# Two-layer graph network on one core: layer 1's products with swapped operands, a constant added by a matrix product, norms by pairs, full-width loads in the sign pass

## The chip, the core and the metric

One core of one Trainium2 chip runs the whole program. The time is device microseconds (us) from launch to end. Three runs of the kernel before gave 795.92, 791.58 and 790.1 us: the median is 791.58 us.

The engines go by their short names: PE (TensorE; its weight loads are shown apart as PEld), DVE (VectorE), ACT (ScalarE), POOL (GpSimd), and SP, which issues plain DMAs. A matrix product has a stationary operand, which is loaded into PE, and a moving operand, whose columns stream through it. "128\*65 128x128 f32" in a group line is a product whose stationary operand is 128 rows by 65 columns and whose moving operand is 128 by 128. A float32 product of this kernel leaves two records in the trace.

## The reference

2708 nodes with 256 features; `adj` is sparse (about 0.3% of its entries and the diagonal are not zero, the first rows and columns hold most). Two layers, each followed by `layernorm(x + layer(x))`:

```
layer 0:  for each of 3 heads: hW = h @ W; e = leaky_relu of sums of hW over neighbours
          att = softmax over j of (e[j] where adj[i, j] > 0); out += (att * adj) @ hW
          two GRU cells (edge, node) on adj @ h and on the mean of the heads;
          result = diag(adj) * (edge cell + node cell)
layer 1:  h = (x @ W) as n x 4 heads x 64
          e[i, j, head] = leaky_relu(s_src[i, head] + s_dst[j, head])   where adj[i, j] > 0.5
          alpha = softmax over i;   out[j] = sum over i of alpha[i, j, head] * h[i, head] + bias
```

A destination j without any entry over 0.5 gets the plain mean over all i: that is what the softmax gives when all its entries are masked alike.

## The kernel before, in words

**Order.** Each operation is first only noted (`Order.add`, lines 100-104) as a node of a graph; nodes held by `together()` stay in one piece. `issue` (line 230) then works out an order for all five engines by a list schedule: a cost in us for each node (`duration`, line 182), a forward pass (line 293) that starts the node of best rank on whichever engine is free first, a backward pass that makes new ranks, and then `tries` = 200 random shifts of ranks, of which the best planned span is kept. In the forward pass a PE node costs twice its duration if it starts between 62 and 146 us, and 1.35 times if it belongs to layer 1 (line 324). The best order is written out; each engine runs its own list strictly in that order. Gathers on POOL are also tied to an operation that the plan has ending shortly before them (lines 406-422).

**Sign pass (0 to about 140 us).** The transposed adjacency is loaded in three column parts (2048 up, 1024 to 2047, 0 to 1023), 22 row blocks each, through a ring of five buffers. ACT writes signs as 8-bit floats into `m8` (22 rows of 2708 bytes per partition, tile f_big); DVE writes "over 0.5" flags (`over`, tile f_wts); PE turns flags into bits (line 956) and multiplies blocks of `m8` with 9 or 18 columns of numbers (`source_products`, line 748). The last column block has only 20 nodes, so its stationary operand has 20 columns.

**Layer 0 (to about 625 us).** For each of six groups of 512 destinations, in the order 4, 3, 2, 1, 0, 5: gathered rows are multiplied and summed, then `cells_and_norm` (line 1193) runs the GRU cells, the norm, writes x1 to X1 (tile f_low), adds it to the running sum `xacc` (line 1271), and writes rows of h, exponentials and bits to the table T1.

**Layer 1 (from about 630 us).** Destinations are cut into 32 pieces (BLOCKS1) 32, 64 or 128 wide. Each has up to 7 lists of 128 sources (tiles). POOL gathers each tile's 128 rows from T1 (`fetch_h`, 96 gathers; a ring of five items of up to three tiles). `layer1` (line 1447) makes a mask (DVE), the weights q = max(S * factor, 1) * mask (the first product on ACT if the piece is 128 wide and its block b is odd, else on DVE; the rest on DVE), and for each tile and head one product: stationary h with a column of ones (65 columns), moving q (32, 64 or 128 columns). So the sums stand with 65 features on the partitions and destinations along the row, in one of three banks `acc`. Of the 104 tiles, 48 are 128 wide, 32 are 64, 23 are 32 and one is 20 wide. When a block of 128 destinations is complete, `finished` (line 1495) adds `hm`, the tiny multiple of the mean of h (four ACT copies, tile f_big), turns the block around with four transposes into a bank `side`, divides by the sum of weights (DVE reciprocal; the multiplication on DVE for odd b, on ACT for even b), adds x1, takes mean and variance, then square root (ACT), reciprocal and shift (DVE), the scaling (ACT), and stores the block. `hm` comes from `xacc` by two small sets of products (lines 1384-1399).

Of the kernel before, what the change touches and what calls it, by code (L numbers as in the profile page):

```python
# [13 lines left out]
F8 = mybir.dt.float8e4  # L14
# [9 lines left out]
P = 128  # L24
# [64 lines left out]
class Order:  # L89
# [3 lines left out]
    def __init__(self, nc, tc):  # L93
        self.tc = tc
        self.nc, self.nodes, self.open, self.held, self.holds = nc, [], None, (), {}
        self.stage, self.stages, self.second, self.tries = None, {}, 1 << 30, 200
        for e in ("tensor", "vector", "scalar", "gpsimd", "sync"):
            setattr(self, e, _Queue(self, e))
# [83 lines left out]
    def duration(self, call):  # L182
# [30 lines left out]
        return 0.45  # L213

    def holds_port(self, call):
# [14 lines left out]
    def issue(self, cross=0.12, pace=0.6, rate=345.0e3, land=2.0, chained=(), turns=12):  # L230
# [55 lines left out]
        port = [self.holds_port(calls[0]) for calls in nodes]  # L286
        gather = [calls[0][1] == "indirect_dma_start" for calls in nodes]
        before = [[] for _ in range(count)]
        for n in range(count):
# [3 lines left out]
        def forward(rank):  # L293
# [11 lines left out]
            for _ in range(count):  # L305
# [82 lines left out]

        chance = random.Random(1)
        parts = sorted(s for s in self.stages if s)  # L390
        for again in range(self.tries):
            moved = list(ahead)
            for part in chance.sample(parts, 3):
                by = chance.uniform(-25.0, 25.0)
                for n in self.stages[part]:
                    moved[n] += by
            rank = [-b - a + chance.uniform(-2.0, 2.0) for b, a in zip(backward(*best[2:]), moved)]
# [49 lines left out]
def fast_path(ctx: ExitStack, tc: tile.TileContext, i: dict, out: bass.AP, bad: bass.AP):  # L447
# [70 lines left out]

    big = Arena("f_big", NB * N)
    wts = Arena("f_wts", 2 * 2 * KD * 3 * D * 4)  # L520
# [173 lines left out]

    G.memset(m8[:, last, :].bitcast(U32), 0)
    G.memset(over_last.bitcast(U32), 0)
# [51 lines left out]
    def source_products(k, bl, lo, hi, end=False):  # L748

        with R.together():  # L750
            for b in bl:
                T.matmul(
                    both[: size[b], b * 2 * H3 + lo : b * 2 * H3 + hi], lhsT=m8[:, k, cols(b)], rhs=u_e[:, k, lo:hi],
                    start=not both_begun[0], stop=end, skip_group_check=True,
                )
                both_begun[0] = True
# [175 lines left out]
    for g, (c0, c1) in enumerate(parts):  # L932
        w = c1 - c0
        b0, b1 = c0 // P, -(-c1 // P)
        for k in range(NB):
# [436 lines left out]
    most = 3  # L1372
    o_ring = Ring([big.take([C65, HEADS1, P], at=4096 + n * 2048) for n in range(2)])
    S_ring = Ring([big.take([P, HEADS1, CH], at=a) for a in (40960, 12288, 28672)])
# [4 lines left out]
    )  # L1379
    hm = home("f_hm", [C65, HEADS1])  # L1380
    V.memset(hm, TINY)
    xm = home("f_xm", [P, KD])
    pm1 = side.next()
# [8 lines left out]
    with R.together():  # L1392
        for h in range(HEADS1):
            for k in range(KD):
                T.matmul(
                    pm2[:C1, h : h + 1], lhsT=w1[:, k, h * C1 : (h + 1) * C1], rhs=xm[:, k : k + 1],
                    start=(k == 0), stop=(k == KD - 1), skip_group_check=True,
                )
    V.tensor_scalar(hm[:C1], pm2[:C1, :HEADS1], TINY, None, op0=MUL)

# [46 lines left out]
    def layer1(j):  # L1447
# [29 lines left out]
        if begin:  # L1477
            outs[b] = acc.next()
            x1b_of[b] = xb_ring.next()
            Q.dma_start(x1b_of[b][: size[b]], X1[b * P : b * P + size[b], :])  # L1480
# [512 lines left out]
```

## Time and profile before

| what | value |
|---|---|
| median of three runs | 791.58 us |
| the profiled execution, its own time | 797.94 us |
| its span, first to last instruction | 796.2 us |
| busy: PE, DVE, POOL, ACT | 652.9, 550.3, 420.3, 261.9 us |
| mean granted PE clock | 0.882 |
| PE busy in 200 to 600 us | 390 of 400 us |
| PE, DVE, POOL, ACT busy in 628 to 782 us | 113.7, 115.2, 103.2, 78.8 of 154 us |

How to read it: each group line gives what one kind of instruction took in all (busy), the mean length of one in ns, and the idle time of its engine just before it with what ended that. The length of one PE record overlaps its neighbours, so prices are taken from whole runs of records (length of the run over its count) or from busy time over count. "PEclk" is the share of PE's full clock that was granted. All operations of the fast path carry line 417, the line that writes the order out, so they are told apart by tile and shape.

### The profile page before, as it was taken

To read this page: it belongs to the slowest core of one execution; us is meant where nothing else is said; L and a number is where in the kernel's file an instruction comes from. 1 tells how busy PE (TensorE), PEld (TensorE's weight loads), DVE (VectorE), ACT (ScalarE), POOL (GpSimd) and SP (SyncE) were. 2 spreads that over 40 slices of the span, in tenths; PEclk is the share of its full clock that TensorE was granted. 3 is DMA by queue.
4 is the path that set the end of the run, shared out by engine and by line. 5 is a ranking of instruction groups with operands and counts; after the bars stand their busy time and mean duration, and the time that the engine had idled before them with its cause. 6 is when DMAs were issued, how large, how long until landed. Compare 5 with 4: busy or idle time off the path is not lost.

```text
span 796.2 us, 12355 instructions
## 1 busy us (share of the span) xinstructions
PE 652.9 (82%) x4212; PEld 467.0 (59%) x4212; DVE 550.3 (69%) x1383; ACT 261.9 (33%) x621; POOL 420.3 (53%) x528
## 2 busy tenths in 40 slices
PE   1786554669999999989999999999998786866763
PEld 1785444555456656565557576574458685755763
DVE  8477798669357968487796455885256585787795
ACT  4436554001113301142114111141225214635775
POOL 5012725546665666576665666763001557777780
PEclk9998555579999999999999999999999756877796
DMA  8888997471114223133213422242004544576541
GB/s 279 327 266 247 320 298 245 144 213 47 39 27 120 77 83 83 42 82 97 53 32 116 126 64 47 54 109 61 1 0 172 195 126 131 180 213 173 142 120 58
DMA packets 60820, 103.68 MB, mean 130 GB/s; under 512 B 20913, under 2 KB 37201, under 8 KB 60109
## 3 DMA queue, kind: packets, MB, share of 16 engines
q1 hardware_dynamic: 40511, 61.62, 23.6%
q0 software_dynamic: 17472, 41.15, 19.9%
q8 instruction: 35, 0.57, 0.3%
q10 hardware_dynamic: 2766, 0.04, 0.2%
q14 instruction: 36, 0.29, 0.1%
HBM read 93.28 MB, written 12.27 MB: 133 GB/s over the span
## 4 chain that ended last, share of the span: by engine, by line
PE 59%; DVE 15%; issue 5%; DMA 5%; ACT 4%; another core or an unknown queue 2%; POOL 1%; SPq 0%; DVEq 0%; ACTq 0%; POOLq 0%
PE side L417 37%; PE acc L417 18%; DVE f_lists L417 4%; ACT f_big L417 3%; DVE f_big L417 3%; DMA f_wts<-in_adjT_dram 3%; PE lst L417 2%; DVE f_low L417 1%; DVE f_raw L417 1%; DMA f_lists<-f_T,f_idx 1%; DVE f_wts L417 1%; DVE f_xT L417 1%; DMA f_xg__139<-f_T,f_idx 1%; SPq L417 0%
## 5 line engine op out<-in xcount | busy, mean ns | idle before, releaser
L417 POOL DMA_INDIRECT f_lists<-f_T,f_idx x96 | 112.6, 1173 | 113.8 <-DMA f_low<-f_X 62.6
L417 POOL DMA_INDIRECT f_raw<-in_adjT_dram,f_idx x115 | 128.5, 1118 | 78.0 <-issue 39.5
L417 PE MATMUL side<-f_xT,f_wts 128*128 128x512 f32 (+1 forms) x288 | 120.6, 544 | 2.6 <-ACT f_big L417 2.6
L417 PE MATMUL side<-f_big,f_wts 128*128 128x512 f32 (+1 forms) x288 | 120.4, 542 | 0.0
L417 PE MATMUL acc<-f_xT,f_lists 128*65 128x128 f32 (+2 forms) x560 | 69.4, 294 | 17.4 <-DVE f_xT L417 13.3
L417 PEld LDWEIGHTS side<-f_big,f_wts 128*128 128x128 f32 x288 | 52.3, 190 | 53.3 <-issue 53.1
L417 PEld LDWEIGHTS side<-f_xT,f_wts 128*128 128x128 f32 x288 | 51.5, 190 | 48.3 <-issue 43.8
L417 PEld LDWEIGHTS acc<-f_xT,f_lists 128*65 128x65 f32 x560 | 65.1, 183 | 20.7 <-DVE f_xT L417 15.4
L417 ACT ACTIVATE f_big<-f_wts 128x1024 fp8e4<-128x1024 f32 (+1 forms) x66 | 60.8, 950 | 39.6 <-DMA f_wts<-in_adjT_dram 26.1
L417 ACT ACTIVATE f_big<-side,f_biases 128x512 f32<-128x512 f32 (+1 forms) x48 | 30.5, 636 | 112.3 <-PE side L417 98.4
L417 PE MATMUL side<-f_pow,f_wts 128*128 128x8 bf16 x484 | 23.8, 170 | 47.3 <-DVE f_wts L417 45.6
L417 PE MATMUL side<-f_big,f_gat_w 128*128 128x512 f32 (+1 forms) x144 | 56.1, 543 | 1.3 <-DVE f_s_d L417 1.3
L417 DVE TENSOR_SCALAR f_wts<-f_wts 128x1024 fp8e4<-128x1024 f32 (+1 forms) x66 | 42.7, 659 | 18.7 <-PE side L417 10.3
L417 PEld LDWEIGHTS <-f_wts 128*128 128x128 fp8e4 x484 | 20.2, 106 | 51.8 <-DVE f_wts L417 48.0
L417 POOL DMA_INDIRECT f_xg__139<-f_T,f_idx x33 | 34.9, 1058 | 27.4 <-issue 7.7
L417 DVE TENSOR_TENSOR f_lists<-f_iota,f_lists 128x2816 f16<-128x2816 f16 (+5 forms) x26 | 48.4, 1862 | 0.6
L417 POOL DMA_INDIRECT f_xg__138<-f_T,f_idx x32 | 36.4, 1137 | 23.3 <-issue 9.0
L417 POOL DMA_INDIRECT f_xg__137<-f_T,f_idx x36 | 35.3, 982 | 25.2 <-issue 9.2
L417 DVE TENSOR_TENSOR f_big<-f_big 128x512 f32<-128x512 f32 (+1 forms) x48 | 30.1, 627 | 24.4 <-ACT f_big L417 22.8
L417 PE MATMUL lst<-f_lists 128*128 128x256 f16 (+4 forms) x285 | 37.8, 296 | 10.0 <-DVE f_lists L417 10.0
L417 POOL DMA_INDIRECT f_xg__140<-f_T,f_idx x30 | 32.6, 1087 | 22.8 <-PE acc L417 8.8
L417 ACT COPY f_big<-acc 128x104 f32<-128x104 f32 (+8 forms) x51 | 12.6, 246 | 95.5 <-PE acc L417 78.5
(260 smaller groups left out, 1275.2 us busy)
## 6 DMA issues: line engine op xcount, KB each, us to landing
f_wts<-in_adjT_dram SPq DMA_DIRECT2D x42, 512.0 KB
f_wts<-in_adjT_dram SPq DMA_DIRECT2D x21, 330.0 KB
f_big<-f_Rd SPq DMA_DIRECT2D x5, 1024.0 KB
f_big<-f_Sd SPq DMA_DIRECT2D x5, 1024.0 KB
f_T<-f_ah SPq DMA_DIRECT2D x21, 132.0 KB
f_X<-f_low SPq DMA_DIRECT2D x21, 128.0 KB
f_low<-f_X SPq DMA_DIRECT2D x21, 128.0 KB
out_dram<-f_big SPq DMA_DIRECT2D x21, 128.0 KB
```

The costliest lines, as they stand in the source:

```text
L417: made[n] = getattr(getattr(self.nc, engine_), method)(*args, **kw)
```

## The change

Six edits, the diff cut to what they do:

1. The planner: PE nodes that start before 160 us cost twice only if an operand of over 48 columns moves (a float32 column counts as 128); layer 1 costs 1.2 times; 280 tries instead of 200, with other random shifts.
2. `m8` gets 108 bytes behind its last row, zeroed with the first 128 columns of every row, and stationary operands of the last column block are read 128 columns wide, over the row's end into the next row. The same for `over`. Rows of the result past the 20th are not used.
3. Layer 1's products change sides: q is stationary (32, 64 or 128 columns) and h with its ones (65 columns) moves. The sums then stand with destinations on the partitions.
4. `hm` becomes one row of 260 numbers, made by two products with one stationary column; it is put into the bank by a first product with a row of ones before a block's other products. The four ACT copies and the four transposes go, and `finished` reads the bank directly.
5. The first multiplication of q goes to ACT for 128-wide pieces with b not divisible by 3, instead of odd b.
6. Square root, reciprocal and shift of the norm are made for two blocks at once (the last four singly); scaling and storing of an even block wait for its neighbour.

```diff
@@ Order
-        self.stage, self.stages, self.second, self.tries = None, {}, 1 << 30, 200
+        self.stage, self.stages, self.second, self.tries = None, {}, 1 << 30, 280
+    def columns(call):
+        moving = call[3]["rhs"] if call[1] == "matmul" else call[2][1]
+        return _size(moving) * (128 if _width(moving.dtype) == 4 else 1)
+        slow = [1.0 + any(self.columns(c) > 48 for c in calls) if e == "tensor" else 1.0 for e, calls in zip(engine, nodes)]
-                    took[n] = busy[n] * (2.0 if 62.0 < t < 146.0 else 1.35 if n >= self.second else 1.0)
+                    took[n] = busy[n] * (slow[n] if t < 160.0 else 1.2 if n >= self.second else 1.0)
-            for part in chance.sample(parts, 3):
-                by = chance.uniform(-25.0, 25.0)
+            wide = chance.choice((3.0, 10.0, 30.0))
+            fine = chance.choice((0.2, 1.0, 4.0))
+            for part in chance.sample(parts, chance.randint(0, 4)):
+                by = chance.uniform(-1.0, 1.0) * wide
@@ sign pass
+    m8_flat = big.take([P, NB * N + SPARE], F8, at=0)
-    G.memset(m8[:, last, :].bitcast(U32), 0)
+    G.memset(m8_flat[:, last * N :].bitcast(U32), 0)
+    G.memset(m8[:, :, : (SPARE + 127) // 128 * 128].bitcast(U32), 0)
-                    both[: size[b], ...], lhsT=m8[:, k, cols(b)], rhs=u_e[:, k, lo:hi],
+                    both[:, ...], lhsT=m8_flat[:, k * N + b * P : k * N + (b + 1) * P],
-                        pb[: size[b], o : o + 8], lhsT=over[:, b * P - c0 : b * P - c0 + size[b]], rhs=pow16,
+                        pb[:, o : o + 8], lhsT=over[:, b * P - c0 : (b + 1) * P - c0], rhs=pow16,
@@ layer 1
-        for h in range(HEADS1):
-            for k in range(KD):
-                T.matmul(pm2[:C1, h : h + 1], lhsT=w1[:, k, h * C1 : (h + 1) * C1], rhs=xm[:, k : k + 1], ...)
-    V.tensor_scalar(hm[:C1], pm2[:C1, :HEADS1], TINY, None, op0=MUL)
+        for k in range(KD):
+            T.matmul(pm2[:1, :D], lhsT=xm[:, k : k + 1], rhs=w1[:, k, :D], start=(k == 0), stop=(k == KD - 1))
+    V.tensor_scalar(hm.rearrange(...)[:, :, :C1], pm2[:1, :D].rearrange(...), TINY, None, op0=MUL)
-        if w == P and b % 2 == 1:
+        if w == P and b % 3:
             outs[b] = acc.next()
+            T.matmul(outs[b][: size[b], :H65], lhsT=ones[:, : size[b]], rhs=hm, start=True, stop=False, ...)
-                        o[:C65, h * P + p0 : h * P + p0 + w], lhsT=hg[:, m, h * C65 : (h + 1) * C65],
-                        rhs=q[:, h, m, :], start=(begin and m == 0 and h == 0),
+                        o[p0 : p0 + w, h * C65 : (h + 1) * C65], lhsT=q[:, h, m, :],
+                        rhs=hg[:, m, h * C65 : (h + 1) * C65], start=False,
@@ finished
-        oc = o_ring.next()
-        for h in range(HEADS1):
-            S.activation(oc[:, h, :p], o[:C65, h * P : h * P + p], AF.Identity, bias=hm[:, h : h + 1])
-        pt = side.next()
-        with R.together():
-            for h in range(HEADS1):
-                T.transpose(pt[:p, h * C65 : (h + 1) * C65], oc[:, h, :p], ident[:C65, :C65])
-        got = pt[:p, :H65].rearrange("p (h c) -> p h c", h=HEADS1)
+        got = o[:p, :H65].rearrange("p (h c) -> p h c", h=HEADS1)
-        S.activation(rstd[:p, b : b + 1], mv[:p, b, 1:2], AF.Sqrt, bias=eps[:p])
-        V.reciprocal(rstd[:p, b : b + 1], rstd[:p, b : b + 1])
-        V.scalar_tensor_tensor(nmr[:p, b : b + 1], mv[:p, b, 0:1], -1.0, rstd[:p, b : b + 1], op0=MUL, op1=MUL)
-        S.activation(y, y, AF.Identity, bias=nmr[:p, b : b + 1], scale=rstd[:p, b : b + 1])
-        Q.dma_start(out[b * P : b * P + p, :], y)
+        waiting.append((b, y))
+        if b % 2 == 0 and b < last - 3:
+            return
+        rstds(waiting[0][0], b + 1)
+        for c, v in waiting:
+            S.activation(v, v, AF.Identity, bias=nmr[: size[c], c : c + 1], scale=rstd[: size[c], c : c + 1])
+            Q.dma_start(out[c * P : c * P + size[c], :], v)
+        waiting.clear()
```

More of the change, by code (lines that the diff above doesn't have):

```diff
@@ L213, in duration @@
         return 0.45
+    @staticmethod
+    def columns(call):
+        moving = call[3]["rhs"] if call[1] == "matmul" else call[2][1]
+        return _size(moving) * (128 if _width(moving.dtype) == 4 else 1)
     def holds_port(self, call):
@@ L387, in issue @@
             rank = [-b - a for b, a in zip(backward(when, took), ahead)]
-        chance = random.Random(1)
+        chance = random.Random(3)
         parts = sorted(s for s in self.stages if s)
@@ L392, in issue @@
             moved = list(ahead)
-            for part in chance.sample(parts, 3):
-                by = chance.uniform(-25.0, 25.0)
+            wide = chance.choice((3.0, 10.0, 30.0))
+            fine = chance.choice((0.2, 1.0, 4.0))
+            for part in chance.sample(parts, chance.randint(0, 4)):
+                by = chance.uniform(-1.0, 1.0) * wide
                 for n in self.stages[part]:
                     moved[n] += by
-            rank = [-b - a + chance.uniform(-2.0, 2.0) for b, a in zip(backward(*best[2:]), moved)]
+            rank = [-b - a + chance.uniform(-fine, fine) for b, a in zip(backward(*best[2:]), moved)]
             for turn in range(3):
@@ L517, in fast_path @@
     X1 = dram.tile([N, D], F32, name="f_X1")
-    big = Arena("f_big", NB * N)
+    SPARE = (NB * P - N + 3) // 4 * 4
+    big = Arena("f_big", NB * N + SPARE)
     wts = Arena("f_wts", 2 * 2 * KD * 3 * D * 4)
@@ L692, in fast_path @@
     early = ah_all[:, : early_n * 64].rearrange("p (s i) -> p s i", i=64)
-    G.memset(m8[:, last, :].bitcast(U32), 0)
+    G.memset(m8_flat[:, last * N :].bitcast(U32), 0)
+    G.memset(m8[:, :, : (SPARE + 127) // 128 * 128].bitcast(U32), 0)
+    for over in over_ring.slots:
+        G.memset(over.bitcast(U32)[:, (N - parts[0][0]) // 4 // 32 * 32 :][:, :32], 0)
     G.memset(over_last.bitcast(U32), 0)
@@ L752, in source_products @@
                 T.matmul(
-                    both[: size[b], b * 2 * H3 + lo : b * 2 * H3 + hi], lhsT=m8[:, k, cols(b)], rhs=u_e[:, k, lo:hi],
+                    both[:, b * 2 * H3 + lo : b * 2 * H3 + hi], lhsT=m8_flat[:, k * N + b * P : k * N + (b + 1) * P],
+                    rhs=u_e[:, k, lo:hi],
                     start=not both_begun[0], stop=end, skip_group_check=True,
@@ L1372, in fast_path @@
     most = 3
-    o_ring = Ring([big.take([C65, HEADS1, P], at=4096 + n * 2048) for n in range(2)])
     S_ring = Ring([big.take([P, HEADS1, CH], at=a) for a in (40960, 12288, 28672)])
@@ L1379, in fast_path @@
     )
-    hm = home("f_hm", [C65, HEADS1])
+    hm = home("f_hm", [1, H65])
     V.memset(hm, TINY)
+    ones = home("f_ones", [1, P])
+    V.memset(ones, 1.0)
     xm = home("f_xm", [P, KD])
@@ L1392, in fast_path @@
     with R.together():
-        for h in range(HEADS1):
-            for k in range(KD):
[L1395 to L1398, printed above, removed]
-    V.tensor_scalar(hm[:C1], pm2[:C1, :HEADS1], TINY, None, op0=MUL)
+        for k in range(KD):
+            T.matmul(pm2[:1, :D], lhsT=xm[:, k : k + 1], rhs=w1[:, k, :D], start=(k == 0), stop=(k == KD - 1))
+    V.tensor_scalar(
+        hm.rearrange("p (h c) -> p h c", h=HEADS1)[:, :, :C1], pm2[:1, :D].rearrange("p (h c) -> p h c", h=HEADS1),
+        TINY, None, op0=MUL,
+    )
     lists.reset()
@@ L1478, in layer1 @@
             outs[b] = acc.next()
+            T.matmul(
+                outs[b][: size[b], :H65], lhsT=ones[:, : size[b]], rhs=hm, start=True, stop=False,
+                skip_group_check=True,
+            )
             x1b_of[b] = xb_ring.next()
@@ L1518, in finished @@
         stats(y, p, b)
-        S.activation(rstd[:p, b : b + 1], mv[:p, b, 1:2], AF.Sqrt, bias=eps[:p])
-        V.reciprocal(rstd[:p, b : b + 1], rstd[:p, b : b + 1])
-        V.scalar_tensor_tensor(nmr[:p, b : b + 1], mv[:p, b, 0:1], -1.0, rstd[:p, b : b + 1], op0=MUL, op1=MUL)
-        S.activation(y, y, AF.Identity, bias=nmr[:p, b : b + 1], scale=rstd[:p, b : b + 1])
-        Q.dma_start(out[b * P : b * P + p, :], y)
+        waiting.append((b, y))
[3 more added lines that the diff above has]
+        for c, v in waiting:
+            S.activation(
+                v, v, AF.Identity, bias=nmr[: size[c], c : c + 1], scale=rstd[: size[c], c : c + 1]
+            )
+            Q.dma_start(out[c * P : c * P + size[c], :], v)
+        waiting.clear()
+    waiting = []
     dn_ring = Ring([home(f"f_dn{n}_", [P, HEADS1]) for n in range(2)])
```

## The prediction

> **What bounds the kernel now.** First the page's slices of the span:
>
> ```profile
> PE   1786554669999999989999999999998786866763
> DVE  8477798669357968487796455885256585787795
> POOL 5012725546665666576665666763001557777780
> PEclk9998555579999999999999999999999756877796
> DMA  8888997471114223133213422242004544576541
> ```
>
> A slice is 19.9 us. In the first seven the adjacency loads set the pace (DMA 8 to 9 tenths) and PE's clock falls to half. In slices 11 to 30 PE is full at full clock: layer 0's work, which the change leaves alone. From slice 32 on no engine is full: layer 1, where the change lies. So I read that stage by itself, cut where the width of the pieces changes (PE, PEld, DVE, ACT and POOL busy us, granted clock, DMA share, GB/s):
>
> ```profile
> 630.00:660.00 30.00, 27.07 (x251) 26.33 (x249) 18.64 (x55) 6.30 (x17) 16.70 (x16) 0.57 0.42 115
> 660.00:676.00 16.00, 9.39 (x96) 8.38 (x94) 11.10 (x30) 8.24 (x24) 11.60 (x11) 0.69 0.56 149
> 676.00:702.00 26.00, 19.43 (x149) 18.16 (x150) 20.68 (x34) 14.66 (x52) 19.11 (x16) 0.86 0.55 165
> 702.00:728.00 26.00, 15.55 (x138) 13.81 (x137) 17.93 (x49) 12.94 (x45) 18.36 (x18) 0.66 0.74 217
> 728.00:782.00 54.00, 40.31 (x308) 38.02 (x307) 45.39 (x96) 36.29 (x128) 36.44 (x26) 0.85 0.45 128
> ```
>
> Narrow pieces (32 and 64 wide) run to 676: PE bounds their first half, at 0.57 of its clock. Then come blocks 3 to 6 (128 wide), 7 to 10 (64 wide), 11 to 20 (128 wide, 5.4 us a block), with PE, DVE and POOL at 67 to 84%. The stage's groups:
>
> ```profile
> L417 POOL DMA_INDIRECT f_lists<-f_T,f_idx x96 | 112.6, 1173 | 113.8 <-DMA f_low<-f_X 62.6 <-issue 16.7 <-PE acc L417 11.7
> ...
> L417 PE MATMUL acc<-f_xT,f_lists 128*65 128x128 f32 x272 | 40.0, 312 | 10.8 <-DVE f_xT L417 8.8 <-issue 1.9
> ...
> L417 ACT ACTIVATE f_big<-acc,f_hm 65x128 f32<-65x128 f32 x84 | 24.2, 362 | 43.7 <-PE acc L417 32.0 <-remote 11.3 <-issue 0.4
> ...
> L417 PE MATMUL side<-f_ident,f_big 65*128 65x65 f32 x84 | 13.5, 268 | 14.8 <-ACT f_big L417 11.0 <-issue 3.6
> ```
>
> Gathers take 1.17 us and stand 0.30 us apart where nothing else holds them: 96 of them need 141 us, and they run from 611.5 to 775.2, 164 us. POOL is the nearest bound, with about 22 us of other waits, of which PE's products are 11.7.
>
> **What a product costs by its two operands.** PE's timeline gives it:
>
> ```profile
> 641.16 2.90 PE L417 MATMUL acc<-f_raw,f_lists 128*65 128x64 f32 x24 [0.94 <-DVE f_raw L417]
> 643.85 1.90 PE L417 MATMUL acc<-f_xT,f_lists 128*65 128x64 f32 x16
> ...
> 651.41 1.87 PE L417 MATMUL side<-f_xm,f_w 128*64 128x1 f32 x16
> 653.20 3.73 PE L417 MATMUL acc<-f_xT,f_lists 128*65 128x32 f32 x32
> ```
>
> All this but the end of the second line is at clock 0.50. 32 moving columns cost 0.11 us a record, and so do 64: with 32 it is the load of 65 columns that counts. 128 moving columns took 3.68 us for 16 at 0.50 (749.7), 0.23 each, and 2.83 for 24 at 1.00 (767.5), 0.118. A record costs the larger of its two sides, about 0.83 ns a column at full clock and 1.67 at half. The nearest row to the new form, a load of 128 with 65 moving, is the transposes: 0.41 us for four at 1.00 (780.6), 0.64 at 0.50 (753.2, the first load hidden).
>
> The swap exchanges the sides, so by the larger side alone no product changes: 128 wide 0.107 at full clock, 0.213 at half; narrow 0.054 and 0.108. What changes is the clock. Cut into steps of 3.4 us, it changes only on their borders, and by what streamed in the step before, not by busy time: from 630.0 to 640.2 PE ran 88 records of 32 columns without a pause, half of each only load, and stayed at 0.50; 40 records of 64 columns from 641.2 to 645.7 brought 1.00. From half clock only steps that streamed over some 82% of what they could were followed by 1.00; at full clock steps of about 40% kept it, and below that it fell. After the change narrow pieces stream all the time (65 moving over loads of 32 or 64), and 128-wide ones half the time.
>
> The Trainium skill, "TensorE: Matmul & The Clock Gate", Part 1, says that full clock comes after one busy window of about 3.4 us and leaves after an idle one. The stretch from 630 to 640 does not agree if busy includes loads. By the page, 128-wide blocks would stay at full clock and the sum below would be about 8 us lower.
>
> **The change part by part**, against the profiled execution (span 796.2, own time 797.9, which is 6.4 above the median).
>
> *Full-width loads in the sign pass:*
>
> ```profile
> L417 PE MATMUL acc<-f_u_e,f_big 128*128 128x9 bf16 x604 | 27.0, 170 | 7.3 <-issue 6.3 <-DVE f_u_e L417 1.0
> ...
> L417 PE MATMUL acc<-f_u_e,f_big 128*20 128x9 bf16 x44 | 7.9, 181 | 0.0
> ...
> L417 PE MATMUL side<-f_pow,f_wts 128*20 128x8 bf16 x22 | 4.0, 181 | 0.0
> ```
>
> 20 columns: 0.18 us a record; 128: 0.045. 66 x 0.135 = 8.9 us of PE, nearly all beside the loads. On the path: 22 records between 49.8 and 57.3 (3.0 us; ACT waits 3.63 us for their result at 58.2, and signs and loads queue behind it) and 8 or 9 after the loads (1.2 us). I take -2, between 0 and -4.2. The zeroing is some 0.7 us (the old one: 0.66) on POOL, which has only such fills until 12.6; the columns it covers are first written at 91 us, so nothing; 0.7 if that cover goes. New wait: the sign of row block k+1 in the last column part comes after the last block's product of row k, as that reads over the row's end. Its weights exist from 93.1, the first sign concerned (block 9) ran at 106.9. 0; if late, ACT's signs and through the ring of five SP's loads wait, up to 3.
>
> *The plan's new order.* The trace cannot show it. Between 200 and 600 PE is idle 10.1 us, which bounds a gain there, and I allow as much loss: 0, -10 to +10.
>
> *`hm` first.* Now each block's first product needs `hm`. In the old order the last piece of `xacc` is added at 646.1 and `hm`'s products end at 653.2, while layer 1 starts at 630.0. If the norm is drawn ahead: last transposes 626.9, statistics 0.6 us twice, table load 1.28, square root 0.29, two small DVE steps 0.3, two scalings 1.0, two sums 0.86, four records 0.56, a copy 0.15, four records of 256 columns at half clock (0.43 each by the column price) 1.7, one DVE step 0.3, handovers: 636. So +6 where PE is the limit; bounds 0 and +23. Behind the waiting product stand all of layer 1's products, then DVE (three q buffers) and POOL (five row buffers).
>
> *Narrow products.* 312 records took 32.7 us (628 to 676). At full clock after two steps of half clock: about 59 x 0.115 + 253 x 0.06 = 22 us. -10.7, of which gathers let me take -7; bounds -10.7 and +4 (loads of 64 columns not quite hidden: list products with 64 stationary columns took 0.128 us at 525.8 to 537.3, those with 128 0.117 at 380.7).
>
> *128-wide products, blocks 3 to 6.* 144 x 0.213 = 30.7 at half clock, and four `hm` products. A record with 264 columns took 0.24 at full clock (2.91 for 12 at 601.6), 0.50 at half (4.01 for 8 at 626.2), so 0.5 to 1.0 a block. Together 34.7 in place of 26 us: +8.7; at full clock 17.4, and POOL's 18 gathers (26 us) bound it: 0. I take the middle, +4.5: the narrow pieces hand over full clock, and it falls when PE catches up (24 x 0.054 us streamed in about 4.5 us a block is 29%, with `hm` 39%).
>
> *Blocks 7 to 10:* POOL and DMA bound them: 0. *Blocks 11 to 20:* at half clock 24 x 0.213 + 1.0 = 6.1 us a block against 5.4: +7; at full clock 3.1 and no bound: 0. I take +4.
>
> *Copies and transposes gone.* PE loses 14.1 us and gains 22 x 0.5 to 1.0 for `hm`; ACT loses 24.9. The chain of waits passes through copies and transposes of finished blocks at 676.8, 685.3, 693.0, 699.4, 709.8 and 717.8, some 9 us; about half returns, as the bank is now held until DVE or ACT has divided: -4, 0 to -9.
>
> *q on ACT, norms by pairs.* Six tiles x 0.586 and nine pairs x 0.31 leave DVE: -6.3 busy; ACT gains 24 x 0.32 = 7.6, which the lost copies cover (without that, ACT would still be under 60%). DVE is at 84% in the last part: -1.5, 0 to -4. An even block's output waits one block, 5.4 us, which its four y buffers cover; SP's row loads queue behind its store, covered by six buffers.
>
> *The end.* From the last product (782.3) copies, transposes and waits until DVE's division take to 787.6; the division now follows the product but for ACT's remaining work: -3.5, -1 to -5.
>
> Sum: -2 + 0 + 6 - 7 + 4.5 + 0 + 4 - 4 - 1.5 - 3.5 = -3.5; the profiled 797.9 becomes 794.4, and the median 791.6 becomes **788**. Little in all, from terms of both signs.
>
> **The rivals.**
> *POOL sets the pace.* The clock holds, or PE's half clock hides in the gathers. For it: POOL's idle after 665 is mostly the bare 0.30. Against: the streaming share above. Half of the 22 us of other waits goes, with the end and the sign pass: -11 - 3.5 - 2 = -16.5, 775.
> *Slower: PE at half clock through every 128-wide block.* The place is 728 to 782: PE needs 61 us where 54 were; with blocks 3 to 6 that is 8.7 + 7 in place of 8.5, and PE at 95% rather than 100% adds 3: 798. It decides from about 60% of these records at 0.50. For it: 0.50 from 630 to 640. Against: blocks 7 to 10 now stream and may restore the clock.
> *`hm` stays late.* The plan leaves the norm behind other work and the first product starts near 653: 17 more; POOL has 13 gathers behind it and needs 83 x 1.47 = 122 us, so the gathers end about as before, plus half the other waits: about +8, 800.
>
> **How the numbers follow.** Chances: likeliest case 0.36 (own range 779 to 797), POOL 0.28 (767 to 783), half clock 0.20 (792 to 805), late `hm` 0.16 (793 to 812). A change under 1% (7.9 us) can't be told from none. Faster takes 0.26 of POOL's case and 0.03 of the likeliest: 0.29. Slower: 0.13 and 0.13 of the last two, 0.03 of the likeliest: 0.29. Same: 0.42. 770 to 806 leaves out half the POOL case's lower part and the upper ends of the last two.
>
> **What would show it.** First layer 1 product at 636 or later, right after `hm`'s products. Narrow records near 0.06 us with clock 1.00 after two steps. 128-wide records at 0.2 us and 0.50 where PE is behind. No 20-column records at 0.18. Under 12 us from last product to end. Wrong if 128-wide blocks hold 1.00 with half the time streamed, or if layer 0's end moves by over 5 us: then the order, not the swap, made the time.

## The result, and the profile after

On the chip that ran both, the changed kernel took 801.63 us (median of four runs, 799.35 to 803.57) and the kernel before 793.75 us (median of four): ratio 1.0101, 95% interval 1.0065 to 1.0138. It is 1% slower. The profiled execution took 803.57 us, with a span of 801.7 us.

PE and its clock, in the slices of the page (20 us each):

```profile
PE   1877455499999999999999999999986767968995
PEclk9996555699999999999999999999999686555555
```

From slice 34 the clock is 6 or 5 tenths to the end, where before it came back to 7 to 9 (6 in the last slice), and in slices 37 to 39 PE is at 8 or 9 tenths, where it had 6 or 7. The stage cut at its own borders (PE, PEld, DVE, ACT and POOL busy us, granted clock, DMA share, GB/s):

```profile
608.60:622.60 14.00, 6.45 (x23) 2.77 (x22) 9.89 (x39) 5.86 (x15) 6.86 (x7) 0.81 0.61 196
622.60:662.30 39.70, 27.78 (x323) 25.42 (x322) 28.17 (x67) 3.85 (x9) 27.67 (x26) 0.76 0.50 132
662.30:697.40 35.10, 30.34 (x151) 28.18 (x150) 21.83 (x41) 14.12 (x48) 20.41 (x19) 0.59 0.48 145
697.40:728.40 31.00, 21.20 (x142) 16.34 (x141) 20.49 (x48) 9.97 (x32) 19.09 (x18) 0.56 0.62 186
728.40:790.40 62.00, 60.49 (x255) 55.30 (x256) 37.15 (x76) 32.72 (x108) 31.14 (x24) 0.50 0.36 101
790.40:801.70 11.30, 2.17 (x13) 0.99 (x12) 3.76 (x17) 2.23 (x5) 0.00 (x0) 0.50 0.11 33
```

Blocks 11 to 20 are the line to read: PE is busy 60.5 of 62.0 us at clock 0.50, and every other engine has a third of the time or more to spare. Beside the kernel before:

| part of the span | before | after | change | predicted |
|---|---|---|---|---|
| to the end of layer 0's last products (128x148) | 622.1 | 608.6 | -13.4 | -2 and 0 ±10 |
| from there to layer 1's first product | 7.9 | 14.0 | +6.0 | +6 |
| blocks 0 to 2 (narrow) | 46.0 | 39.7 | -6.3 | -7 |
| blocks 3 to 6 (128 wide) | 26.0 | 35.1 | +9.1 | +4.5 |
| blocks 7 to 10 (64 wide) | 26.0 | 31.0 | +5.0 | 0 |
| blocks 11 to 20 (128 wide) | 54.0 | 62.0 | +8.0 | +4 |
| the end | 14.2 | 11.3 | -2.9 | -3.5 |
| sum | 796.2 | 801.7 | +5.5 | -3.5, with -5.5 not tied to a part |

So two large things cancel: layer 0 ends 13.4 us earlier, and all behind it takes 193 us where it took 174. The cells' first products in layer 0 and its last, before (L417) and after (L427):

```profile
188.67 1.88 PE L417 MATMUL side<-f_xT,f_wts 128*128 128x512 f32 x4
176.95 1.98 PE L427 MATMUL side<-f_xT,f_wts 128*128 128x512 f32 x4
621.41 0.67 PE L417 MATMUL side<-f_big,f_wts 128*128 128x148 f32 x4
607.97 0.67 PE L427 MATMUL side<-f_big,f_wts 128*128 128x148 f32 x4
```

PE's timeline after:

```profile
621.45 1.23 PE L427 MATMUL acc<-f_hm,f_ones 1*128 1x260 f32 x2 [0.50 <-DVE f_hm L427]
622.61 5.29 PE L427 MATMUL acc<-f_lists,f_xT 128*32 128x65 f32 x48
...
642.76 1.82 PE L427 MATMUL acc<-f_lists,f_xT 128*32 128x65 f32 x32
...
672.33 5.38 PE L427 MATMUL acc<-f_lists,f_raw 128*128 128x65 f32 x24 [4.76 <-DVE f_raw L427]
...
739.98 5.38 PE L427 MATMUL acc<-f_lists,f_xT 128*128 128x65 f32 x24
745.29 1.23 PE L427 MATMUL acc<-f_hm,f_ones 1*128 1x260 f32 x2
746.45 5.38 PE L427 MATMUL acc<-f_lists,f_xT 128*128 128x65 f32 x24
```

The first product comes right behind `hm`. The narrow records take 1.82 / 32 = 0.057 us at clock 1.00. From 739.98 a block takes 6.47 us with no bracket behind any line, so PE waits for nothing: 24 records in 5.31 and the product with the mean in 1.16. The groups of the stage:

```profile
L427 POOL DMA_INDIRECT f_lists<-f_T,f_idx x96 | 110.8, 1154 | 131.1 <-ACT f_big L427 68.1 <-issue 17.9 <-PE acc L427 15.8
L427 PE MATMUL acc<-f_lists,f_xT 128*128 128x65 f32 x272 | 56.4, 398 | 0.0
...
L427 PE MATMUL acc<-f_hm,f_ones 1*128 1x260 f32 x42 | 21.9, 624 | 4.2 <-DVE f_big L427 2.1 <-ACT f_big L427 1.6 <-DVE f_hm L427 0.5
```

The same 272 records took 40.0 us before. The mean's 21 products cost 21.9 us, 1.04 each; the transposes had cost PE 14.1. The chain of waits, with its long pieces from 662 on:

```profile
663.09 6.09 DMA f_lists<-f_T,f_idx
...
672.33 24.18 PE acc L427 x104
696.51 6.49 DMA f_lists<-f_T,f_idx
...
728.39 42.88 PE acc L427 x178
...
774.79 17.61 PE acc L427 x82
```

PE's products are the chain from 672 to 697 and, but for 3.5 us, from 728 to 792.

### The profile page after: what moved, and what is told of

It reads as the page before. It is cut to its first block, busy times and chain, and to the rows that moved or that the text cites. A ratio compares the mean times of both kernels' runs of the same rounds, so it can differ in the third digit from the quotient of the medians.

```text
span 801.7 us, 12180 instructions
## 1 busy us (share of the span) xinstructions
PE 671.3 (84%) x4156; PEld 475.5 (59%) x4156; DVE 547.5 (68%) x1364; ACT 245.6 (31%) x548; POOL 422.7 (53%) x532
## 4 chain that ended last, share of the span: by engine, by line
PE 63%; DVE 11%; DMA 6%; issue 3%; ACT 2%; SPq 1%; POOL 0%; another core or an unknown queue 0%; ACTq 0%; DVEq 0%; POOLq 0%
PE side L427 36%; PE acc L427 24%; PE lst L427 3%; DVE f_big L427 3%; DVE f_lists L427 3%; DMA f_lists<-f_T,f_idx 2%; DVE f_raw L427 2%; DMA f_big<-f_Sd 1%; DMA f_xg__138<-f_T,f_idx 1%; DVE f_xT L427 1%; ACT L427 1%; SPq L427 1%; DMA f_wts<-in_adjT_dram 1%; DVE f_wts L427 1%; ACT f_big L427 0%
## 5 line engine op out<-in xcount | busy, mean ns | idle before, releaser
L427 POOL DMA_INDIRECT f_lists<-f_T,f_idx x96 | 110.8, 1154 | 131.1 <-ACT f_big L427 68.1
L427 POOL DMA_INDIRECT f_raw<-in_adjT_dram,f_idx x115 | 121.5, 1056 | 77.0 <-issue 39.2
L427 PE MATMUL side<-f_xT,f_wts 128*128 128x512 f32 (+1 forms) x288 | 120.1, 543 | 0.1
L427 PE MATMUL side<-f_big,f_wts 128*128 128x512 f32 (+1 forms) x288 | 119.8, 542 | 0.0
L427 PE MATMUL acc<-f_lists,f_xT 128*128 128x65 f32 (+2 forms) x560 | 83.6, 335 | 7.0 <-issue 5.6
L427 PEld LDWEIGHTS acc<-f_lists,f_xT 128*128 128x128 f32 (+2 forms) x560 | 80.0, 238 | 14.6 <-issue 8.0
L427 PEld LDWEIGHTS side<-f_big,f_wts 128*128 128x128 f32 x288 | 52.1, 190 | 53.5 <-issue 53.1
L427 PEld LDWEIGHTS side<-f_xT,f_wts 128*128 128x128 f32 x288 | 51.7, 190 | 45.4 <-issue 43.5
L427 ACT ACTIVATE f_big<-f_wts 128x1024 fp8e4<-128x1024 f32 (+3 forms) x66 | 61.0, 951 | 42.7 <-DMA f_wts<-in_adjT_dram 24.9
L427 ACT ACTIVATE f_big<-side,f_biases 128x512 f32<-128x512 f32 (+1 forms) x48 | 30.4, 635 | 124.6 <-PE side L427 107.3
L427 PE MATMUL side<-f_pow,f_wts 128*128 128x8 bf16 x484 | 20.2, 169 | 52.8 <-DVE f_wts L427 51.5
L427 POOL DMA_INDIRECT f_xg__137<-f_T,f_idx x36 | 43.6, 1210 | 27.4 <-PE acc L427 8.1
L427 PE MATMUL side<-f_big,f_gat_w 128*128 128x512 f32 (+1 forms) x144 | 56.4, 543 | 0.0
L427 PE MATMUL acc<-f_lists,f_raw 128*64 128x65 f32 (+3 forms) x272 | 41.5, 337 | 17.3 <-DVE f_raw L427 17.3
L427 DVE TENSOR_SCALAR f_wts<-f_wts 128x1024 fp8e4<-128x1024 f32 (+3 forms) x66 | 47.8, 736 | 8.7 <-DMA f_wts<-in_adjT_dram 8.6
L427 PEld LDWEIGHTS acc<-f_lists,f_raw 128*64 128x64 f32 (+3 forms) x272 | 39.0, 244 | 22.3 <-DVE f_raw L427 20.6
L427 PEld LDWEIGHTS <-f_wts 128*128 128x128 fp8e4 x484 | 17.9, 107 | 56.8 <-DVE f_wts L427 54.2
L427 DVE TENSOR_TENSOR f_lists<-f_iota,f_lists 128x2816 f16<-128x2816 f16 (+5 forms) x26 | 48.3, 1866 | 0.3
L427 POOL DMA_INDIRECT f_xg__138<-f_T,f_idx x32 | 38.4, 1201 | 18.8 <-issue 5.7
L427 POOL DMA_INDIRECT f_xg__140<-f_T,f_idx x30 | 34.3, 1144 | 21.6 <-issue 9.8
L427 POOL DMA_INDIRECT f_xg__139<-f_T,f_idx x33 | 34.9, 1057 | 18.6 <-issue 6.2
L427 DVE TENSOR_TENSOR f_big<-f_big 128x512 f32<-128x512 f32 (+1 forms) x48 | 30.2, 629 | 20.6 <-ACT f_big L427 15.6
```

Of the source, the lines that this page charges most:

```text
L427: made[n] = getattr(getattr(self.nc, engine_), method)(*args, **kw)
```

## The experiments

Theory 1: the swap halves the columns that stream in a 128-wide block (65 moving over a load of 128), the clock goes by streamed columns, and so PE stays at 0.50. Theory 2: the new order makes the time. Theory 3: the mean costs it, by its products or by the wait for it. The chips differ by some 2% (the kernel before took 779 us on the chip of five runs: old sides, columns twice, mean on 4 columns, loads alone, and the mean that waits for nothing; 796 us on the chips of the others), so ratios are compared, and absolute times only on one chip. Times in the expectations of those five are meant for the slower chip: 784 us, say, is a ratio of 0.985.

### Old sides, all else changed

```diff
-                        o[p0 : p0 + w, ...], lhsT=q[:, h, m, :], rhs=hg[...], start=False,
+                        o[:C65, ...], lhsT=hg[...], rhs=q[:, h, m, :], start=(begin and m == 0 and h == 0),
```
with the old `hm`, copies and transposes; edits 1, 2, 5 and 6 stay. The order is planned anew.

> The changed kernel with layer 1's products, the four ACT copies, the transposes and the mean as they were before (edits 3 and 4 undone; planner, full-width loads, q on ACT and norms by pairs kept; the order is planned anew). Theory 1 (half clock: 128-wide swapped products hold PE at 0.50, which costs 8 us in blocks 11 to 20 and as much in blocks 3 to 6, where the changed kernel starts layer 1 earlier than before): layer 0 still ends about 10 us earlier, blocks 11 to 20 take 54 us again; 784 us, 0.985 to 0.995 of before. Theory 2 (the new order lost the time, the swap is harmless): stays at 798 us or above. Theory 3 (the first products' wait for the mean and their own 1.2 us lost it): as theory 1, so this run does not tell 1 from 3.

Ratio 1.0042 (1.0015 to 1.0069), mean clock 0.899 against 0.851 with the swap. The clock is back, but the time is not below that of the kernel before, where theory 1 had 0.985 to 0.995; it is what theory 2 had (798 us or more, a ratio of 1.003 or more). In this order layer 0 ends at 613.4 us, 11 us later than kernels with the changed kernel's order do on the same chip (602.8 and 602.3 below). Behind layer 0 it takes 167.5 us, where the swapped kernel with the mean's product on 4 columns (below, same chip) takes 182.7. Undoing the swap also threw away the order, so this run bears out the clock and leaves the price in the whole time open.

### Stream the 65 columns twice

Same order as the changed kernel; each 128-wide product moves its columns a second time, into columns of the bank that nobody reads.

```diff
-    o[p0 : p0 + w, h * C65 : (h + 1) * C65], ..., rhs=hg[:, m, h * C65 : (h + 1) * C65],
+    twice(o, h), ..., rhs=hg[:, m, h * C65 : (h + 1) * C65].unsqueeze(1).to_broadcast([P, 2, C65]),
```

> The changed kernel in its own order, instruction for instruction, but each 128-wide product moves its 65 columns twice (130 moving columns over 128 loaded), the second time into unused columns of the bank: more work on PE, which fills the half of each record in which nothing streamed. Theory 1: two steps of 3.4 us after the first dense stretch the clock is 1.00 and stays near it while PE is behind; records fall from 0.224 to about 0.115 us, blocks 11 to 20 from 62 to 50 to 55 us, the whole to 780 to 790 us. Theory 2 and theory 3: the clock does not follow what streams, records stay at 0.22 or grow, 801 to 806 us.

Ratio 0.9939 (0.9907 to 0.997), so faster than both. Blocks in its timeline, and its stretch of blocks 11 to 20:

```profile
719.45 2.96 PE L427 MATMUL acc<-f_lists,f_xT 128*128 128x130 f32 x24
722.34 0.70 PE L427 MATMUL acc<-f_hm,f_ones 1*128 1x260 f32 x2
722.99 2.96 PE L427 MATMUL acc<-f_lists,f_xT 128*128 128x130 f32 x24
```

```profile
715.00:761.20 46.20, 39.33 (x255) 35.27 (x256) 36.51 (x76) 31.67 (x106) 30.02 (x24) 0.86 0.47 133
```

With twice the columns, 24 records take 2.96 us instead of 5.38, and the mean clock of the stretch is 0.86 instead of 0.50. Nothing else was changed. Work that is thrown away brings the clock, and the clock takes away more than the work costs: theory 1.

### The mean's product on 4 columns

Same order; the product with the mean moves only the four columns of the sums of weights, so the mean of h is left out for destinations without entries.

```diff
-    outs[b][: size[b], :H65], lhsT=ones[:, : size[b]], rhs=hm,
+    four_(outs[b][: size[b]]), lhsT=ones[:, : size[b]], rhs=four_(hm),
```

> The changed kernel in its own order, but the first product of each block moves 4 columns (those of the ones) instead of 260, so the mean of h is left out for destinations without entries. Theory 3: the 22 products cost 1.2 us each on the path, 14 of them where PE has no pause: 12 to 17 us less, 785 to 789 us, with the clock at 0.50 as before. Theory 1: the same where PE is the limit, as each 128-wide block takes 5.4 in place of 6.5 us; it differs in that the records stay at 0.224 and that the gain ends at the pace of 5.4 us a block. Theory 2: within 2 us of 801.

```profile
667.56 7.09 PE L427 MATMUL acc<-f_lists,f_xT 128*128 128x65 f32 x32
674.58 0.58 PE L427 MATMUL acc<-f_hm,f_ones 1*128 1x4 f32 x2
```

Ratio 1.0062 (1.0033 to 1.0092), against 1.0101 for the full product: the intervals overlap. 256 columns less shorten the product from 1.23 to 0.58 us at half clock; the records stay at 0.22 us. Blocks 11 to 20 take 58.7 us from their first record to the last block's mean, where the changed kernel takes 62.0: of the 8 us lost there the mean's columns are some 3. Theory 3's 12 to 17 us did not come, and the clock is still 0.851.

### Full-width loads alone, and the planner alone

Edit 2 alone on the kernel before, and edit 1 alone.

```diff
-    both[: size[b], ...], lhsT=m8[:, k, cols(b)],
+    both[:, ...], lhsT=m8_flat[:, k * N + b * P : k * N + (b + 1) * P],
```

> The kernel before with only the full-width loads of the sign pass (edit 2), its order planned anew by the old planner. No 20-column record of 0.18 us is left. If those loads brought layer 0's earlier end (13 us in the last cells' products): 779 to 785 us. If the planner brought it: within 4 us of before.

```diff
-    took[n] = busy[n] * (2.0 if 62.0 < t < 146.0 else 1.35 if n >= self.second else 1.0)
+    took[n] = busy[n] * (slow[n] if t < 160.0 else 1.2 if n >= self.second else 1.0)
```

> Only the planner's edit on the kernel before: new search, new seed, TensorE's costs doubled for wide products before 160 us. Layer 1 keeps its old sides and finish. Theory of the order (the new order is what brought layer 0's end forward in the changed kernel): the last 128x148 product ends some 8 to 13 us earlier than in the kernel before and the time falls, ratio 0.985 to 0.995. Rival (any new order moves the stages by chance, as the run with the loads alone did by +1.9%): the ratio lies anywhere from 0.99 to 1.02 and layer 0 ends within 5 us of before.

Ratios 1.0185 (1.0136 to 1.0235) and 1.0084 (1.0056 to 1.0111): both slower, by the place where layer 0 ends (620.8 on the faster chip, 620.1 on the slower) and by what follows. The first is outside both of its expectations. Neither edit by itself brings the early end of layer 0. In the changed kernel's own order it ended at 608.6, 609.1, 606.1 and 611.3 in the four profiles on the slower chips and at 602.8, 602.3 and 601.4 on the faster; every other order ended it later: 612.0 to 622.1 on the slower, 613.4 and 620.8 on the faster. So the 13 us go with the order (that of the last run below comes near it), and with no edit that I could show: the run with the old sides has the same layer 0 and the same edits there, and ends it 11 us later. The planner's run fell out as its rival had it: layer 0's end within 5 us of before.

### The sides alone

Edits 3 and 4 alone, with the old planner, loads, ACT's share and single norms.

> Only the swap of sides with the mean's product and the finish without copies and transposes; the old planner, loads, ScalarE's share and single norms. Theory of the clock: the 128-wide blocks run at a granted clock of 0.50 throughout, 24 records in 5.3 to 5.4 us and the mean's product in 1.2 us, 6.4 to 6.6 us a block from block 11 to 20, and the ratio is 1.005 to 1.02. Rival (the order and the other edits cost the time, the swap itself is free): blocks 11 to 20 in 5.4 us each and the ratio within 0.5% of 1 or below.

Ratio 1.0149 (1.01 to 1.0199). Its last blocks:

```profile
740.00:800.00 60.00, 57.28 (x241) 50.48 (x240) 40.11 (x89) 27.12 (x88) 27.14 (x21) 0.50 0.34 97
```

Another order, and again 0.50 and PE full to the end: 24 records in 5.38 us, a mean's product in 1.23. The slow stage belongs to the swap, not to the order.

### Stream half of the products twice

As above, but only heads 1 and 3 move their columns twice.

```diff
-    twice(o, h) if w == P else ...
+    twice(o, h) if w == P and h % 2 else ...
```

> As the run that streams the 65 columns twice in every 128-wide product, but in two of the four products of a chunk only, so 97.5 columns a product on average; same order as the changed kernel. Theory of the clock with the bound read off the trace of before (about 82% of what half clock can stream): loads of 0.213 us hide the columns, so a pair streams for 0.217 + 0.108 of 0.43 us, 76%; the clock stays at 0.50, 24 records take 5.2 to 5.6 us, and the ratio stays that of the changed kernel, 1.005 to 1.012. Rival (any streaming above that of the changed kernel is enough): steps at 1.00 appear in the stretch of blocks 11 to 20, and the ratio is below 1.0.

Ratio 0.9906 (0.9872 to 0.994): the expectation of theory 1 failed and its rival's came. Steps of 3.4 us, cut at the clock's own borders (the last one 0.1 us inside them; same columns as above):

```profile
681.10:684.50 3.40, 3.40 (x16) 3.40 (x17) 0.42 (x1) 0.00 (x0) 1.74 (x2) 0.50 0.63 180
684.50:687.90 3.40, 3.40 (x18) 3.40 (x16) 3.04 (x5) 2.86 (x12) 1.66 (x1) 0.50 0.13 27
742.50:745.90 3.40, 3.40 (x18) 3.33 (x16) 3.37 (x6) 2.36 (x7) 2.71 (x3) 0.50 0.75 219
745.90:749.30 3.40, 3.09 (x24) 2.56 (x23) 1.95 (x5) 3.23 (x12) 2.92 (x2) 1.00 0.44 109
715.29:718.55 3.26, 3.26 (x23) 2.48 (x22) 2.58 (x6) 1.64 (x7) 2.24 (x2) 0.50 0.34 112
```

My 76% was right, and the bound of 82% was not. The view counts every record that reaches into a step; of the 18 at 742.5 two had begun before it. The 16 that begin in it move 130 and 65 columns, 8 each: 1560 columns x 1.67 ns = 2.60 us, 76% of a step, and the next one runs at 1.00. So it went in all four steps of this kind (684.5, 728.9, 742.5 and 766.4). The step at 681.1, with 15 such records (73%), was followed by 0.50. The changed kernel's steps hold 16 records of 65, 51%, and never get there. By this the border lies near 75%.

Steps with a mean's product do not fit. That at 715.2 holds 20 records of 65 columns and the mean's two of 260, 89% with these and 63% without, and the next one stayed at 0.50. In the changed kernel the step at 716.4 holds 18 records of 65 and two of 260, 1690 columns or 83% (57% without), and stayed too, where in the same order 26 ordinary records of 65, again 1690 columns, brought 1.00 (647.5, in the run below in which the mean waits for nothing). So the product with one row seemed not to count; that got runs of its own.

### The mean over 128 rows

The order of the run with half, and that of the run with all products doubled, with the mean's product spread over 128 rows, the same sum in the bank.

```diff
-    hm = home("f_hm", [1, H65]);  V.memset(hm, TINY);      ones = home("f_ones", [1, P])
+    hm = home("f_hm", [P, H65]);  V.memset(hm, TINY / P);  ones = home("f_ones", [P, P])
-    T.matmul(pm2[:1, :D], lhsT=xm[:, k : k + 1], ...
+    T.matmul(pm2[:, :D], lhsT=xm[:, k : k + 1].to_broadcast([P, P]), ...
```

> The run that streams half of the 128-wide products twice, in the same order, with the mean's product spread over 128 rows (the mean over 128 in every row, against a block of ones), where it had one row; the sum that it puts into the bank is the same. In that run the half-clock steps without a mean's product that streamed 83% or more of what half clock allows were followed by 1.00, and three steps at 92 to 98% with one to three mean's products among them were not. Theory that a product of one row counts little for the clock: steps at 0.50 that hold a mean's product are now followed by 1.00, the stretch of blocks 11 to 20 (728 to 777 there) gets 3 to 6 us shorter, and the ratio falls from 0.991 to 0.983 to 0.988. Rival (columns count whatever their rows): the same pattern of the clock and 0.987 to 0.994.

> The run that streams all 128-wide products twice, in the same order, with the mean's product over 128 rows. Theory that a one-row product counts little for the clock: fewer steps at 0.50 than in that run from block 11 on, so 1 to 4 us less, ratio 0.988 to 0.993 (0.994 there). Rival: nothing changes, 0.991 to 0.997.

Ratios 0.9851 (0.9823 to 0.9879) and 0.9842 (0.9791 to 0.9892), against 0.9906 and 0.9939 with one row. Both pairs gained, by 0.6 and 1.0%, as the theory had it, but the intervals of the first pair overlap, and the two runs of the second were on chips of different speed. Two steps of the first (cut 0.2 us before the clock's borders):

```profile
672.70:676.10 3.40, 3.40 (x17) 3.40 (x17) 1.86 (x4) 3.40 (x13) 2.58 (x3) 0.50 0.49 138
676.10:679.50 3.40, 3.40 (x30) 3.32 (x29) 2.62 (x4) 1.72 (x6) 2.91 (x2) 0.98 0.59 172
```

Block 4 starts at 670.6 and has full clock from 676.3, 5.7 us on; with one row it started at 674.3 and got full clock at 687.9, and blocks 3 to 6 took 30.2 us where they now take 28.2 (first record to the next block's mean). In the step at 672.9 seven records of 130 columns, six of 65 and the first of the mean's begin: 76% with the mean's and 64% without, so here the mean's columns seem to count. But it is one step, near the border, and where the block falls on the clock's steps moves the shares too: the cause is not settled. The place in the expectation was wrong too: blocks 11 to 20 take as long as before (49 and 48 us), although the clock rose from 0.74 to 0.79, as PE no longer sets their pace (41 of 49 us busy). And some 3 us of the 6.9 in the spans is layer 0's end, 606.1 against 609.1 in the same order. That these two are the fastest kernels here, 2.5% below the changed one, is measured; that one-row products do not count for the clock is borne out by the steps above and not shown.

### The mean last

The run that streams twice, and in blocks 0 to 2 the bank begun with zeros and the mean added last.

```diff
+        if b < 3:
+            T.matmul(o[:p, :H65], lhsT=ones[:, :p], rhs=hm, start=False, stop=True, ...)
```

> The run that streams twice, with one thing more: in blocks 0 to 2 the bank is begun by a product with a row of zeros, and the mean's product is added last. Theory that layer 1's first product waits for the chain of the mean (12 to 14 us behind the last cells): the first layer-1 product starts 4 to 7 us earlier after the last 128x148 product than in the run without this, and the ratio falls from 0.994 to 0.986 to 0.991. Rival (gathers of T land no earlier, so that the wait is only renamed): the first product may come earlier, but blocks 3 to 6 start at the same time, and the ratio stays 0.991 to 0.997.

Ratio 0.9985 (0.9964 to 1.0007), outside both expectations. The first product comes 7.7 us behind layer 0's last instead of 14.0, but the edit made a new order, in which layer 0 ends at 617.7. From there to the end it takes 178.4 us, as long as the run with half the products doubled (178.3). It speaks against a price of the wait, but through another order.

### The mean waits for nothing

The changed kernel's order kept instruction by instruction: the order is planned as before, and only when it is written out do the mean's products get other operands, which have long been there. The mean is left out, and a row of W1 stands in its place in the sums.

```diff
-            for engine_, method, args, kw in nodes[n]:
+            for engine_, method, args, kw in map(self.other, nodes[n]):   # xacc, xm: identity; hm: a row of W1
```

> The changed kernel in its own order, with the waits for the mean taken from TensorE: the three steps of the mean's chain read data that has long been there (the identity for the sums of X and for the mean of X, a row of W1 for TINY x mean h), so nothing that TensorE issues waits for that chain. The sums in the banks get a wrong term: the mean is left out and a row of W1 is in its place. Theory that the wait for the mean costs its full stretch: the first layer-1 product starts 7 to 9 us earlier (some 613 to 615 where it was 622.6) and the end comes 5 to 8 us earlier, ratio 1.000 to 1.004 against 1.010. Rival (behind it stand the masked values on VectorE, at 619.6 for the second chunk, and the gathers, which end the wait before block 3 at 672 in either case): the first product starts earlier but the products from 672 on start within 2 us of where they did, and the ratio is 1.006 to 1.012.

Its timeline, and then that of the run with the mean's product on 4 columns (the same order and a chip as fast):

```profile
609.69 4.63 PE L427 MATMUL acc<-f_lists,f_xT 128*32 128x65 f32 x48
...
661.05 5.39 PE L427 MATMUL acc<-f_lists,f_raw 128*128 128x65 f32 x24 [5.26 <-DVE f_raw L427]
```

```profile
661.73 5.38 PE L427 MATMUL acc<-f_lists,f_raw 128*128 128x65 f32 x24 [5.70 <-DVE f_raw L427]
```

Layer 1's first product starts at 609.7, where it was at 614.3 there, and block 4's at 661.1 against 661.7. The ratio is 1.0148 (1.0115 to 1.0182), not below that of the changed kernel and a little above the rival's 1.012. The wait for the mean is real and costs nothing at the end: behind it stands the wait for gathered rows, which ends when it did (the last gather on the chain before block 4 lands at 658.8 here and at 658.6 there).

### Only the narrow blocks swapped

```diff
+    wide = set(range(3, 7)) | set(range(11, 21))      # old sides, copies and transposes for these
```

> As the changed kernel, but the 128-wide blocks (3 to 6 and 11 to 20) keep the sides of before, with their copies and transposes at the end and the mean added in the copies; only blocks 0 to 2 and 7 to 10 are swapped. The order is planned anew. Theory of the clock (the swap costs time in the 128-wide blocks alone): from block 11 on records at 1.00, 5.2 to 5.5 us a block or less, and the stretch from the last 128x148 product to the end takes 170 to 178 us (193 in the changed kernel, 174 in the kernel before); ratio 0.98 to 1.005 by where its order puts the end of layer 0. Rival (the narrow swap costs too): 180 us or more for that stretch and a ratio over 1.005.

Ratio 0.9984 (0.9954 to 1.0014). From layer 0's end to the end it takes 182 us, which was the rival's number, but 19.6 of these pass before the first product at 631.5: the second form of the mean takes 1.9, and the sum over x1 that both need is there 13.6 us behind layer 0's last product, where it was there after 8.3 in the changed kernel. From the first product on it takes 162.5 us, where the kernel before takes 166.2 and the changed one 179.1, and the 128-wide blocks have their clock back (0.84 from 732 to 782):

```profile
735.59 2.78 PE L427 MATMUL acc<-f_xT,f_lists 128*65 128x128 f32 x24
```

By this the narrow swap does no harm; whether it gains, with two orders apart by more than 4 us, stays open.

## Why the prediction was wrong, step by step

- *128-wide blocks, +4.5 and +4: the steps that failed.* They measured +9.1 and +8.0. Both bounds were right but for 1 us, and I took the middle. The rule that I had read off the trace (82% of a step streamed) gives 51% for these blocks and so 0.50 throughout; the hope that the 64-wide blocks would hand over full clock came true for one step (702.7 to 706.1) and not up to block 11. The 82% itself was too high: the trace before has no step at 0.50 in layer 1 between 68 and 81%, and 76% was enough in a run above. The rival at half clock had its place and price right: 18.7 us for its parts, 17.1 measured. It should have been the likeliest case. Within it the block was 6.47 us, not 6.1: the mean's product was 1.16, over my bound of 1.0, and a record 0.221, not 0.213.
- *Blocks 7 to 10, 0:* +5.0. Kernels with the same order and a higher clock before them took 29.0 to 32.0 us too, so it is not the clock alone; the chain there goes through a gather (6.49 us) and a load of S (5.29, from 708.0). Which part of the change brought it was not tried.
- *The order, 0 and ±10:* -13.4, outside the bounds. I bounded it by PE's idle time between 200 and 600, but the first 600 us also hold the loads: the cells' first product started at 177.0 instead of 188.7, so most of the gain was there before layer 0's bulk began. That the whole came out only 1% slower is luck: without these 13 us, for which the sum had 0, it would be about 815 us. My mark for a wrong reading (layer 0's end moves by over 5 us, so the order made the time) came up and misled by half: the order gave 13 us, and the swap took 17.
- *`hm` first, +6:* the chain took 14.0 us behind the last cells; 622.1 to 636 was predicted. As a cost it was none, by the run in which the mean waits for nothing.
- *Narrow products, -7:* -6.3, with 0.057 us a record at 1.00.
- *Full-width loads, -2:* the 20-column records are gone (11.9 us of PE), but alone the edit was 1.9% slower in its order. Open.
- *Copies gone, q on ACT, norms by pairs, -4 and -1.5:* where PE is full at 0.50, DVE has 37 busy us of 62 and ACT 33, so they can bring little there; no run tried them alone. With the clock back, blocks 11 to 20 take 46 to 49 us against 54, which holds what they and the swap bring together.
- *The end, -3.5:* -2.9; 9.3 us from last product to end, as said under 12.
- *POOL sets the pace:* wrong; POOL is busy 31 of the last blocks' 62 us.

The Trainium skill, "TensorE: Matmul & The Clock Gate", Part 1, gives full clock after a busy window of 3.4 us. PE was busy 60.5 of 62.0 us, loads included, and stayed at 0.50; doubling the streamed columns alone brought 1.00. The measurement decides: busy time is not what counts here.

## What to carry to other kernels

When the sides of a product are swapped, price the clock with it: count the columns that stream in a step of 3.4 us beside those that are loaded (here, from half clock, 73% of a step was too little and 76% enough). Where a load of 128 columns hides a stream of 65, streaming something useless beside it can be faster. Before an edit is judged in a kernel whose order is searched, compare where the unchanged part ends: here that alone moved by 13 us.

## What was not expected of the hardware

- A product with one row and 260 float32 columns took 1.23 us at clock 0.50 and 0.70 at 1.00 (4 columns: 0.58 and 0.38), about the time with 128 rows (1.24 and 0.60 to 0.71). Two steps that came to 83 and 89% only with such products stayed at 0.50, where 83% of ordinary records brought 1.00; whether the single row is the reason stays open.
- Layer 0's end varied by 5 us between profiles of one order (606.1 to 611.3), and the same kernel by 2% between chips.
